# The last batch tile in six output groups, one of them stored through GpSimd's queue on 15 DMA engines

## The chip, the cores and the metric

The kernel runs on one core of one Trainium2 chip. Five engines work beside each other on that core: TensorE (PE) multiplies matrices into PSUM, VectorE (DVE), ScalarE (ACT) and GpSimd (POOL) do elementwise work, and SyncE (SP) here only issues transfers. Sixteen DMA engines move bytes between SBUF and HBM. A transfer is issued by SP, ACT or GpSimd[...].

The metric is the device time of one execution in microseconds (us). The kernel before took 1342.57 us, the median of three runs (1342.16 to 1344.26).

## What is computed

```python
# x: (4096, 32, 64) f32     W: (496, 64, 64) f32     out: (4096, 496, 64) f32
idx_i, idx_j = np.triu_indices(32, k=1)        # the 496 pairs i < j
vi = inputs[:, idx_i, :]
vj = inputs[:, idx_j, :]
vidots = jnp.einsum('bpd,pde->bpe', vi, W)     # one 64x64 matrix for each pair
return vidots * vj
```

For each batch row and each pair (i, j), field i is multiplied by the pair's own matrix and the product is multiplied elementwise with field j. The output is 496 x 64 floats for each of 4096 rows: 520 MB, against 34 MB of input and 8 MB of weights.

## The kernel before

The batch is cut into 32 tiles of 128 rows (tile t is block t // 2, half t % 2). For each tile the 496 pairs go through 46 steps: a step is one field i and up to CH = 16 of its partners j. TensorE writes a step's products into one of four PSUM buffers, then VectorE multiplies them with field j into an output buffer `ot`; for seven of the steps ScalarE copies PSUM out and GpSimd multiplies.

The steps are gathered into groups, and each group has one `ot` buffer and one store. There are three such buffers, so group n can only be written when the store of group n - 3 has landed, on all DMA engines.

```python
    CH = BANK // E2                                             # 16
    p0 = [i * (F - 1) - i * (i - 1) // 2 for i in range(F)]     # first pair of field i
    bounds = [0, p0[3], p0[6] + CH, p0[11], p0[17], NP]         # 0, 90, 187, 286, 391, 496
    groups = list(zip(bounds[:-1], bounds[1:]))                 # 90, 97, 99, 105, 105 pairs
    cap = max(b - a for a, b in groups)
    aside = (1, 3, 5, 7, 9, 11, 13)
    ...
    opool = ctx.enter_context(tc.tile_pool(name="opool", bufs=3))
    psum = ctx.enter_context(tc.tile_pool(name="psum", bufs=4, space=bass.MemoryType.PSUM))
```

Stores go out by SP's queue, one transfer per group: 128 rows, and for each row one contiguous run of pairs (105 pairs are 26,880 bytes). Most loads of x go by ACT's queue. Every third block's load goes by GpSimd's queue instead, in the form that the change takes up: 120 rows in one transfer and the other 8 rows in two more. Small dummy transfers (`turn_engines`) stand between them[...].

```python
    SWR = 120
    ...
    def turn_engines(k: int):
        n = k if k > 1 else 17
        c = used[0] % 8
        used[0] += 1
        src = x[: NB * n].rearrange("(p k) f d -> p k f d", k=NB)
        tc.keep_in_program_order(
            nc.gpsimd.dma_start(out=scratch[:n, :, c : c + 1], in_=src[:, :, 0, 0:1])
        )

    def load_fifteen(blk: int):
        ...
        part(slice(0, SWR), slice(0, F))
        turn_engines(1)
        for h in range(2):
            part(slice(SWR, P), slice(h * F // 2, (h + 1) * F // 2))
    ...
    turn_engines(5)                       # once, at the start
```

The main loop, cut to what the change touches:

```python
    for s, (t, st) in enumerate(sched):
        blk, kt = divmod(t, NB)
        g, i, c0, m = steps[st]           # group, field, first partner, partners
        ...
        base, end = groups[g]
        pa = p0[i] + c0
        if pa == base:
            ots[t] = opool.tile([P, cap, D], F32, tag="ot", name=f"ot_{t}_{g}")
        ot = ots[t]
        ...                               # matmuls into ps
        o = pa - base
        dst = ot[:, o : o + m, :].rearrange("p m (h e) -> p m h e", h=2)
        ...
        if i in aside and c0 == 0 and s not in no_aside:
            tmp = tpool.tile([P, CH, 2, E2], F32, tag="tmp", name=f"tmp_{s}")
            nc.scalar.copy(tmp, src)
            nc.gpsimd.tensor_mul(dst, tmp, xj)
        else:
            nc.vector.tensor_mul(dst, src, xj)
        ...
        if pa + m in ends:
            n0 = ...
            nc.sync.dma_start(
                out=rows_of(out, blk).rearrange("(p k) n d -> p k n d", k=NB)[:, kt, n0 : pa + m, :],
                in_=ot[:, n0 - base : pa + m - base, :],
            )
    turn_engines(11)                      # once, at the end
```

Of the kernel before, what the change touches and what calls it, by code (L numbers as in the profile page):

```python
# [12 lines left out]
def kernel(  # L13
# [16 lines left out]
    nc = tc.nc  # L30

    B, F, D = x.shape
    P = 128
    NB = 2
    assert 2 * D == P and B % (NB * P) == 0
    NBLK = B // (NB * P)
    NP = F * (F - 1) // 2
    E2 = D // 2
    BANK = 512
    CH = BANK // E2  # L40
    RUN = 8
    p0 = [i * (F - 1) - i * (i - 1) // 2 for i in range(F)]


    bounds = [0, p0[3], p0[6] + CH, p0[11], p0[17], NP]
    groups = list(zip(bounds[:-1], bounds[1:]))
    cap = max(b - a for a, b in groups)

    aside = (1, 3, 5, 7, 9, 11, 13)

# [15 lines left out]
    def rows_of(dram: bass.AP, blk: int) -> bass.AP:  # L66
        return dram[blk * NB * P : (blk + 1) * NB * P]

    def new_x(blk: int):

        wide = xpool.tile([P, NB, F * D + 16], F32, tag="xs", name=f"xs_{blk}")
        xs[blk] = wide[:, :, : F * D].rearrange("p k (f d) -> p k f d", d=D)

    def load_x(blk: int, eng, k0: int = 0, k1: int = NB):
        src = rows_of(x, blk).rearrange("(p k) f d -> p k f d", k=NB)
        eng.dma_start(out=xs[blk][:, k0:k1], in_=src[:, k0:k1])
# [4 lines left out]
    SWR = 120  # L81
# [4 lines left out]
# [10 lines that stand above are left out]
        rows = rows_of(x, blk).rearrange("(p k) f d -> p k f d", k=NB)  # L96
        dst = xs[blk]

        def part(ps: slice, fs: slice):
            tc.keep_in_program_order(nc.gpsimd.dma_start(out=dst[ps, :, fs, :], in_=rows[ps, :, fs, :]))  # L100

        part(slice(0, SWR), slice(0, F))
        turn_engines(1)
        for h in range(2):
            part(slice(SWR, P), slice(h * F // 2, (h + 1) * F // 2))


    wflat = w.rearrange("p d e -> p (d e)")
    raw, wT = {}, {}
# [3 lines left out]
    def load_w(c: int, eng=nc.sync):  # L113

        a, b = wrows[c]
        pool, tag = ((opool, "ot"), (opool, "ot"), (const, "w3"), (const, "w3"))[c]
        raw[c] = pool.tile([P, D * D], F32, tag=tag, name=f"raw_{c}")
        eng.dma_start(out=raw[c][: b - a, :], in_=wflat[a:b])

    def order_w(c: int, k: int, copy):  # L120
        r = wrows[c][1] - wrows[c][0]
        rp = tpool.tile([P, EU, 2, D], F32, tag="tmp", name=f"rp_{c}_{k}")
        src = raw[c][:r, :].rearrange("p (d h e) -> p e h d", h=2, d=D)
        copy(rp[:r], src[:, k * EU : (k + 1) * EU])  # L124
        return rp

    def turn_w(c: int, k: int, rp, copy):
        r = wrows[c][1] - wrows[c][0]
        home, tag, n = (wrows[c][0], "w3", r) if c == 3 else (0, "w", wrows[3][0])
        if home not in wT:  # L130
            wT[home] = const.tile([P, n, E2], F32, tag=tag, name=f"wT_{home}")
        pt = psum.tile([P, EU, P], F32, tag="ps", name=f"ptw_{c}_{k}")
        for n in range(EU):
            nc.tensor.transpose(  # L134
                pt[:, n, :r], rp[:r, n].rearrange("p h d -> p (h d)"), ident[:r, :r]
            )
        o = wrows[c][0] - home
        copy(wT[home][:, o : o + r, k * EU : (k + 1) * EU], pt[:, :, :r].rearrange("p e r -> p r e"))  # L138

    def turn_x(blk: int, k: int, q: int, copy):  # L140


        pt = psum.tile([P, RUN // 2, P], F32, tag="ps", name=f"ptx_{blk}_{k}_{q}")
        for u in range(RUN // 2):
            f = q * RUN + 2 * u
            nc.tensor.transpose(  # L146
                pt[:, u, :], xs[blk][:, k, f : f + 2, :].rearrange("p f d -> p (f d)"), ident
            )
        xT = xtpool.tile([P, 2, RUN // 2, P], F32, tag="xT", name=f"xT_{blk}_{k}_{q}")
        copy(xT[:, 0], pt)  # L150
        copy(xT[D:, 1], pt[:D])  # L151
        copy(xT[:D, 1], pt[D:])  # L152
        return xT


    steps = [
        (g, i, c0, min(CH, F - 1 - i - c0))
        for i in range(F - 1)
        for c0 in range(0, F - 1 - i, CH)
        for g, (a, b) in enumerate(groups)  # L160
        if a <= p0[i] + c0 < b
    ]
    NS = len(steps)
    first = {}
    for s, (_, i, _, _) in enumerate(steps):
# [5 lines left out]
    NT = NBLK * NB  # L171
# [36 lines left out]
    v, p, a = nc.vector.tensor_copy, nc.gpsimd.tensor_copy, nc.scalar.copy  # L208
# [8 lines left out]
    ots = {}  # L217
    for s, (t, st) in enumerate(sched):
        blk, kt = divmod(t, NB)
        g, i, c0, m = steps[st]  # L220
        if s in loads:
            new_x(loads[s])
            if loads[s] % 3 == 0:
                load_fifteen(loads[s])
            else:
                load_x(loads[s], nc.scalar)
        for what, *args in due.get(s, ()):
            if what == "x":
                xT[tuple(args)] = turn_x(*args, a)
            elif what == "turn":  # L230
                turn_w(*args, rps.pop(tuple(args)), a)
            else:
                c, k = args
                rps[c, k] = order_w(c, k, (v, v, p, v)[c] if k % 2 == 0 else (v, v, p, a)[c])
                if (c, k) == (2, NU - 1):
                    load_w(3, nc.scalar)

        base, end = groups[g]
        pa = p0[i] + c0
        if pa == base:  # L240
            ots[t] = opool.tile([P, cap, D], F32, tag="ot", name=f"ot_{t}_{g}")
        ot = ots[t]
        ps = psum.tile([P, 2, CH, E2], F32, tag="ps", name=f"ps_{s}")
        for lo, hi in ((0, wrows[3][0]), wrows[3]):
            home, lo, hi = lo, max(pa, lo), min(pa + m, hi)
            if lo < hi:
                for h in range(2):
                    nc.tensor.matmul(  # L248
                        ps[:, h, lo - pa : hi - pa, :],
                        xT[blk, kt, i // RUN][h * D : (h + 1) * D, (i + h) % 2, i % RUN // 2, :],  # L250
                        wT[home][h * D : (h + 1) * D, lo - home : hi - home, :],
                        start=True,
                        stop=True,
                    )
        o = pa - base
        j = i + 1 + c0
        dst = ot[:, o : o + m, :].rearrange("p m (h e) -> p m h e", h=2)
        src = ps[:, :, :m, :].rearrange("p h m e -> p m h e")
        xj = xs[blk][:, kt, j : j + m, :].rearrange("p m (h e) -> p m h e", h=2)
# [7 lines that stand above are left out]
        ends = (p0[2], end) if s < NS and (t, g) == (0, 0) else (end,)  # L267
        if pa + m in ends:
            n0 = p0[2] if len(ends) > 1 and pa + m == end else base
            nc.sync.dma_start(  # L270
                out=rows_of(out, blk).rearrange("(p k) n d -> p k n d", k=NB)[:, kt, n0 : pa + m, :],
                in_=ot[:, n0 - base : pa + m - base, :],
            )
    turn_engines(11)


# [25 lines left out]
```

## Time and profile before

| | |
|---|---|
| time, median of 3 runs | 1342.57 us |
| span of the profiled execution | 1341.7 us |
| busy: PE / DVE / ACT / POOL | 85% / 71% / 35% / 40% |
| bytes moved, mean rate | 562.86 MB, 420 GB/s |
| written to HBM | 520.09 MB |
| share of the 16 DMA engines' time by SP's queue (q1) | 93.0% |
| by ACT's queue (q10) / GpSimd's queue (q0) | 3.8% / 2.0% |
| chain that ended last: DMA / PE / DVE / POOL | 55% / 22% / 14% / 5% |

In the profile's page, the span is cut into 40 equal slices of 33.5 us; a digit is the busy share of a slice in tenths. A transfer is made of packets, and each packet runs on one of the 16 DMA engines. "Landing" is the moment when the last engine of a transfer reports its part as written. The chain is followed back from the last instruction, at each step to whatever released it.

### The profile page before, as it was taken

How to read it: one execution, taken by the hardware profiler on the slowest of the kernel's cores; microseconds unless marked ns; L12 is line 12 of the kernel's file. 1: busy time of each engine (PE TensorE's matmuls, PEld its weight loads, DVE VectorE, ACT ScalarE, POOL GpSimd, SP SyncE). 2: the span in 40 equal slices, each digit the busy share in tenths (PEclk: the TensorE clock that was granted, in tenths of full speed). 3: DMA queues.
4: the chain of work that ended last, by engine and by line, in shares of the span. 5: the costliest groups of instructions: out<-in, count | busy, mean ns of one | idle time of the engine just before them, and what ended most of it. 6: DMA issues, size and time to landing. Idle time of an engine off the chain costs nothing.

```text
span 1341.7 us, 16676 instructions
## 1 busy us (share of the span) xinstructions
PE 1137.5 (85%) x6656; PEld 605.0 (45%) x6656; DVE 954.2 (71%) x1262; ACT 467.7 (35%) x623; POOL 543.0 (40%) x252
## 2 busy tenths in 40 slices
PE   5989888878798797998888988788897879988884
PEld 3545444444344444444444544344444435444442
DVE  4778777767677676776767777577775767777774
ACT  4443333333233342333333333333333323333331
POOL 1723343444334443343453434434334433444441
PEclk9989999989999898998999999899998999999997
DMA  9899999999999999999999999999999999999997
GB/s 383 347 428 419 418 425 427 431 422 430 422 432 431 420 430 421 431 424 432 424 415 430 421 432 426 417 430 408 425 429 429 427 421 428 418 416 431 429 432 320
DMA packets 28895, 562.86 MB, mean 420 GB/s; under 512 B 3537, under 2 KB 3537, under 8 KB 3825
## 3 DMA queue, kind: packets, MB, share of 16 engines
q1 hardware_dynamic: 24176, 530.59, 93.0%
q10 hardware_dynamic: 2576, 20.71, 3.8%
q0 software_dynamic: 2064, 10.50, 2.0%
q8 instruction: 52, 0.85, 0.2%
q14 instruction: 27, 0.21, 0.0%
HBM read 41.68 MB, written 520.09 MB: 419 GB/s over the span
## 4 chain that ended last, share of the span: by engine, by line
DMA 55%; PE 22%; DVE 14%; POOL 5%; issue 2%; ACT 1%; SPq 0%; DVEq 0%; POOLq 0%; ACTq 0%
DMA out_dram<-ot 53%; PE ps L248 20%; DVE ot L265 13%; POOL ot L263 4%; DMA xs<-in_r_inputs_dram 2%; PE ptx L146 2%; ACT tmp L262 1%; PE ptw L134 1%; DVE rp L124 0%; POOL rp L124 0%; ACT xT L150 0%; ACT xT L152 0%; ACT xT L151 0%; DVEq L265 0%; POOL xs L100 0%
## 5 line engine op out<-in xcount | busy, mean ns | idle before, releaser
L265 DVE TENSOR_TENSOR ot<-ps,xs 128x1024 f32<-128x1024 f32 (+15 forms) x1252 | 940.9, 807 | 357.1 <-DMA out_dram<-ot 214.9
L248 PE MATMUL ps<-wT,xT 64*128 64x512 f32 (+13 forms) x6016 | 1046.1, 488 | 167.9 <-DVE ot L265 163.3
L263 POOL TENSOR_TENSOR ot<-tmp,xs 128x1024 f32<-128x1024 f32 x220 | 519.4, 2362 | 770.7 <-ACT tmp L262 592.6
L248 PEld LDWEIGHTS ps<-wT,xT 64*128 64x128 f32 x6016 | 534.7, 195 | 620.3 <-DVE ot L265 372.8
L262 ACT COPY tmp<-ps 128x1024 f32<-128x1024 f32 x220 | 222.7, 1012 | 498.0 <-PE ps L248 462.5
L150 ACT COPY xT<-ptx 128x512 f32<-128x512 f32 x128 | 74.9, 585 | 322.8 <-PE ptx L146 322.8
L146 PE MATMUL ptx<-ident,xs 128*128 128x128 f32 x512 | 84.8, 289 | 13.8 <-DMA xs<-in_r_inputs_dram 8.8
L146 PEld LDWEIGHTS ptx<-ident,xs 128*128 128x128 f32 x512 | 54.2, 142 | 85.9 <-DVE ot L265 60.0
L152 ACT COPY xT<-ptx 64x512 f32<-64x512 f32 x128 | 74.5, 582 | 1.5
L151 ACT COPY xT<-ptx 64x512 f32<-64x512 f32 x128 | 73.9, 577 | 1.5
L134 PE MATMUL ptw<-ident,rp 128*128 128x128 f32 (+1 forms) x128 | 19.1, 304 | 4.8 <-DVE rp L124 4.8
L134 PEld LDWEIGHTS ptw<-ident,rp 128*128 128x128 f32 (+1 forms) x128 | 16.1, 160 | 12.5 <-issue 5.4
L138 ACT COPY wT<-ptw 128x1024 f32<-128x1024 f32 (+1 forms) x15 | 14.8, 984 | 20.0 <-PE ptw L134 16.1
L124 DVE COPY rp<-raw 128x1024 f32<-128x1024 f32 (+1 forms) x9 | 12.8, 1453 | 10.6 <-DMA raw<-in_L_rec_W_dram 10.6
L100 POOL DMA_DIRECT2D xs<-in_r_inputs_dram x15 | 9.5, 636 | 0.0
L124 POOL COPY rp<-raw 128x1024 f32<-128x1024 f32 x4 | 8.0, 1990 | 0.1
L124 ACT COPY rp<-raw 112x1024 f32<-112x1024 f32 (+1 forms) x3 | 5.8, 1949 | 4.6 <-POOL ot L263 2.7
L92 POOL DMA_DIRECT2D scratch<-in_r_inputs_dram x7 | 6.2, 888 | 0.3 <-issue 0.3
L138 DVE COPY wT<-ptw 128x1024 f32<-128x1024 f32 x1 | 1.2, 1224 | 2.5 <-PE ptw L134 2.5
L150 ACT ACT_TABLE_LOAD x1 | 1.3, 1283 | 0.7 <-PEq L289 0.7
masks.py:199 POOL TENSOR_SCALAR_AFFINE_SELECT ident<-ident 128x128 f32<-128x128 f32 x1 | 0.3, 292 | 0.1
masks.py:197 POOL MEMSET ident<- 128x128 f32 x1 | 0.2, 204 | 0.3 <-POOLq L289 0.3
(4 smaller groups left out, 0.4 us busy)
## 6 DMA issues: line engine op xcount, KB each, us to landing
out_dram<-ot SPq DMA_DIRECT2D x64, 3360.0 KB, 16.4
out_dram<-ot SPq DMA_DIRECT2D x32, 3168.0 KB, 15.9
out_dram<-ot SPq DMA_DIRECT2D x32, 3104.0 KB, 17.0
out_dram<-ot SPq DMA_DIRECT2D x31, 2880.0 KB, 16.9
xs<-in_r_inputs_dram ACTq DMA_DIRECT2D x9, 2048.0 KB, 25.4
xs<-in_r_inputs_dram POOLq DMA_DIRECT2D x5, 1920.0 KB, 25.0
raw<-in_L_rec_W_dram SPq DMA_DIRECT2D x3, 2048.0 KB, 13.8
xs<-in_r_inputs_dram SPq DMA_DIRECT2D x2, 1024.0 KB, 10.3
```

Of the source, the lines that this page charges most:

```text
L100: tc.keep_in_program_order(nc.gpsimd.dma_start(out=dst[ps, :, fs, :], in_=rows[ps, :, fs, :]))
L124: copy(rp[:r], src[:, k * EU : (k + 1) * EU])
L134: nc.tensor.transpose(pt[:, n, :r], rp[:r, n].rearrange("p h d -> p (h d)"), ident[:r, :r])
L138: copy(wT[home][:, o : o + r, k * EU : (k + 1) * EU], pt[:, :, :r].rearrange("p e r -> p r e"))
L146: nc.tensor.transpose(pt[:, u, :], xs[blk][:, k, f : f + 2, :].rearrange("p f d -> p (f d)"), ident)
L150: copy(xT[:, 0], pt)
L151: copy(xT[D:, 1], pt[:D])
L152: copy(xT[:D, 1], pt[D:])
L248: nc.tensor.matmul(ps[:, h, lo - pa : hi - pa, :], xT[blk, kt, i // RUN][h * D : (h + 1) * D, (i + h) % 2, i % RUN // 2, :], wT[home][h * ...
L262: nc.scalar.copy(tmp, src)
L263: nc.gpsimd.tensor_mul(dst, tmp, xj)
L265: nc.vector.tensor_mul(dst, src, xj)
```

## The change

Only the last of the 32 tiles is altered. Its pairs are cut into six groups instead of five: 90, 97 and 99 pairs as before, then 55, 100 and 55 in place of 105 and 105. The fifth group, of 100 pairs, is stored by GpSimd's queue instead of SP's, in two transfers: rows 0 to 119, which are to fall on 15 DMA engines, and rows 120 to 127, one row on each of 8. It is meant to leave out of the larger part the one DMA engine that lags behind the rest, as the loads of every third block do. Each row goes as two runs of 50 pairs, so that its pieces are near in size to those of the 55-pair stores; to keep the two runs apart, the second half is written one pair further on in the buffer. [...]

```diff
+    last = [*bounds[:4], p0[13] + CH, p0[21], NP]
+    last_groups = list(zip(last[:-1], last[1:]))
+    HALVED = 4
+    half = p0[17] - last[HALVED]
+    assert last[HALVED + 1] == p0[17] + half
     cap = max(b - a for a, b in groups)
+    assert 2 * half + 1 < cap
 ...
+    def store_fifteen(dram: bass.AP, ot: bass.AP):
+        dst = dram.rearrange("p (c n) d -> p c n d", c=2)
+        src = ot[:, : 2 * half + 2, :].rearrange("p (c n) d -> p c n d", c=2)[:, :, :half, :]
+        for rows in (slice(0, SWR), slice(SWR, P)):
+            tc.keep_in_program_order(nc.gpsimd.dma_start(out=dst[rows], in_=src[rows]))
 ...
-        g, i, c0, m = steps[st]
+        g, i, c0, m = (last_steps if t == NT - 1 else steps)[st]
 ...
-        base, end = groups[g]
+        base, end = (last_groups if t == NT - 1 else groups)[g]
+        halved = (t, g) == (NT - 1, HALVED)
 ...
-        o = pa - base
+        o = pa - base + (halved and pa - base >= half)
 ...
-            nc.sync.dma_start(
-                out=rows_of(out, blk).rearrange("(p k) n d -> p k n d", k=NB)[:, kt, n0 : pa + m, :],
-                in_=ot[:, n0 - base : pa + m - base, :],
-            )
-    turn_engines(11)
+            dram = rows_of(out, blk).rearrange("(p k) n d -> p k n d", k=NB)[:, kt, n0 : pa + m, :]
+            if halved:
+                store_fifteen(dram, ot)
+                turn_engines(4)
+            else:
+                nc.sync.dma_start(out=dram, in_=ot[:, n0 - base : pa + m - base, :])
```

## The prediction

> **What bounds the kernel now.** I read the busy times first, then the slices, then the end of the chain, then the stretches of the last 40 us.
>
> ```profile
> PE 1137.5 (85%) x6656; PEld 605.0 (45%) x6656; DVE 954.2 (71%) x1262; ACT 467.7 (35%) x623; POOL 543.0 (40%) x252
> ...
> DMA  9899999999999999999999999999999999999997
> GB/s 383 347 428 419 418 425 427 431 422 430 422 432 431 420 430 421 431 424 432 424 415 430 421 432 426 417 430 408 425 429 429 427 421 428 418 416 431 429 432 320
> ```
>
> No compute engine is full, but the DMA digit is 9 in nearly every slice at about 425 GB/s: the store of 520 MB sets the pace, and the only slack that a change in the last tile can reach lies in the last slice, at 320 GB/s. If that slice (33.5 us) ran at 425 GB/s it would be about 8 us shorter, part of which is the last latency and teardown. That is already below 2% of the time (26.9 us).
>
> The stretches of the end say how the slack is spread over the engines (columns: start and end, length, five engines, clock, DMA share, GB/s):
>
> ```profile
> 1324.50:1325.30 0.80, 0.00 (x0) 0.00 (x0) 0.00 (x0) 0.00 (x0) 0.00 (x0) 1.00 0.71 302
> 1325.30:1333.20 7.90, 0.00 (x0) 0.00 (x0) 0.00 (x0) 0.00 (x0) 0.00 (x0) 0.51 0.98 419
> 1333.40:1336.20 2.80, 0.00 (x0) 0.00 (x0) 0.00 (x0) 0.00 (x0) 0.00 (x0) 0.50 0.11 48
> 1336.40:1339.50 3.10, 0.00 (x0) 0.00 (x0) 0.00 (x0) 0.00 (x0) 0.00 (x0) 0.50 0.06 26
> 1339.60:1341.70 2.10, 0.00 (x0) 0.00 (x0) 0.00 (x0) 0.00 (x0) 0.00 (x0) 0.50 0.02 4
> ```
>
> From 1325.3 to 1333.2 all 16 DMA engines carry the last store; then the share is 0.11, two engines of 16, and from 1336.4 it is 0.06, a single one. Put packet to packet, the trace gives the same: the last store's data ends between 1333.26 and 1334.19 on fourteen engines, at 1336.28 on one, and at 1339.53 on the last, called B here. B is 6.2 us behind the crowd. The 26,880-byte packet takes 996 ns on B too, so B isn't slow at the end: it brought the lag along. Hence the purpose of the change: give B less.
>
> The chain shows what else hangs on B:
>
> ```profile
> 1299.26 17.00 DMA out_dram<-ot
> 1316.26 0.03 issue
> 1316.29 0.05 DVEq L265
> 1316.34 0.04 issue
> 1316.39 7.86 DVE ot L265 x13
> 1324.25 0.13 DVEq L298
> ```
>
> The store of the 97 pairs (187 less 90) lands at 1316.26 because B ends its part at 1315.75; the others were through by about 1311. Only then is a buffer free for the fifth group, VectorE fills it until 1324.38, SP issues at 1324.41, and the first packet runs at 1325.29, 0.88 us later. The crowd ends the fourth group's 105 pairs at 1324.5 to 1325.7, so it hardly idles. B runs from 1315.75 through three stores without a gap: 23.78 us to 1339.53.
>
> [...] in each of the five split loads one engine gets only completion packets of 4 bytes where 15 get sixteen 8,192-byte packets each. Across the load at 1176, B's lag on the stores falls from about 5 to about 3 us, so the engine left out is B. [...] I take it that B is left out again, and that B is the first of the 8 engines of the second part.
>
> [...] In the split loads 8,192-byte packets of q0 stand between q1's stores, so two queues share an engine and neither stops. [...]
>
> ```profile
> 1172.19 0.78 POOL L100 DMA_DIRECT2D xs<-in_r_inputs_dram  x1
> 1172.97 0.98 POOL L92 DMA_DIRECT2D scratch<-in_r_inputs_dram  x1
> ...
> 1314.08 0.59 POOL L92 DMA_DIRECT2D scratch<-in_r_inputs_dram  x1
> ```
>
> The first q0 packet of the load issued at 1172.19 runs at 1175.74, 3.55 us later; the three loads before it need 3.5, 3.6 and 3.9, the very first 5.2. The dummy transfer of 1314.08 shows its first packet at 1316.51, 2.4 us later. The measured figures are used.
>
> **The change part by part.** Nothing before 1308.8 alters. I write times on the profile's scale.
>
> Packets: 23,040 bytes take 855 ns and 26,880 take 996, so 36.7 ns per KB (1,000 bytes) and some 9 ns fixed. A row of 55 pairs (14,080 bytes) is 526 ns, half a row of 100 pairs (12,800 bytes) 479 ns.
>
> 1. Fourth group, 55 pairs. Its buffer is free at 1308.76 as before, its last product is GpSimd's of 1311.79 to 1314.15, so its store goes out some 1.2 us sooner than the 105 pairs did. Crowd: eight packets, 4.2 us after the 99 pairs (ended 1316.4 to 1317.8): through at about 1320.6 to 1322. B: 99 pairs end at 1323.55 as before, then 4.2 us: 1327.8.
> 2. Fifth group, 100 pairs. It still waits for the landing at 1316.26. VectorE: 2, 16, 1, 16, 15, 14, 13, 12 and 11 pairs, at 0.28, 1.22, 0.21, 1.22, 1.15, 1.09, 1.01, 0.95 and 0.88 us (rows of the same shapes), 8.01 in sum; successive ones overlap by 0.077 each (the fourteen before add up to 9.07 and took 7.99), so 7.4 us: 1316.39 to 1323.8.
> 3. GpSimd's issue: about 1323.9; with 3.45 us to the first packet, 1327.35. The load of 120 rows with two runs per row has as many pieces, which is why I take its latency and not the dummy's. The crowd therefore stands idle from about 1321 to 1327.35, where before it waited about half a microsecond. This is the cost of the change.
> 4. Sixth group, 55 pairs. Buffer free when the 99 pairs land, B's 1323.55, landing 1324.07. VectorE's ten steps of 10 to 1 pairs add up to 5.14, less nine overlaps, 4.45 us: 1324.2 to 1328.65; SP's first packet 0.9 us later, 1329.55. It comes before q0 is empty, so it adds work but no gap.
> 5. The end. Engines with 8 rows of the 100 pairs: 16 x 0.479 + 8 x 0.526 = 11.87 us, 1339.2. The seven besides B with a ninth row: 18 x 0.479 + 8 x 0.526 = 12.83 us, 1340.2. B: one row, 0.96, and 4.2 of the sixth group: about 1334. The engine at 1336.28 before is through with its fourth group at 1324.6, and its lag vanishes in the idle stretch.
>
> Before, data ended at 1339.53; after, at 1340.2: about 0.65 us later. Both hang on the same moment, B's 1315.75, and so differ by 23.78 against 24.4 us (0.51 landing, 0.13 to VectorE, 7.4, 0.1 to the issue, 3.45, 12.83) however far B lags. The teardown after the last landing, 1339.99 to 1341.7, stays. Time: 1342.57 + 0.65, or 1343.2 us.
>
> **The rivals.** *The intended gain.* If the lag were simply shared out, sixteen engines would all end near the present mean of 1333.9, 5.6 us sooner: 1337 us. For it speaks that B does get 0.96 instead of 7.7 us. Against it: bytes can be shared only when there are bytes to send, and between 1321 and 1327 there are none for the crowd, as the fifth group's buffer waits for B.
>
> *GpSimd's transfer starts quicker on idle engines.* With the dummy's 2.4 us, data ends at 1339.15: 1342.2 us. [...] Against: the wait for a packet in progress is at most 1 us on one engine, and with fifteen engines the first one opens almost at once.
>
> *GpSimd's path is worse for stores.* Rows of 12,800 bytes are longer than any that q0 carries in this trace; if they are cut smaller or take longer to prepare, or if the landing of a store by q0 is reported later, 1 to 2 us come on top: 1344 to 1345 us.
>
> *B isn't the engine left out.* Then B gets eight rows, 1327.8 + 11.9 = 1339.7, or 1340.6 with nine; no worse than the crowd, and the time is again 1343 us.
>
> **Range and chances.** All ways lie within 1337 and 1345 us. The term with the widest doubt is the 3.45 us, which I think may be 2.4 to 4.5; the three runs of before spread over 2.1 us. So 1341.4 to 1344.9. A step past 2% would need 26.9 us, which the last tile doesn't hold.
>
> **What would show it.** The first q0 data packet of the store near 1327.3 and a hole in the DMA share from about 1321; VectorE's idle stretch before 1316.4, 1.02 us now, some 4 to 5 us longer; seven engines that end last, together, about a microsecond after the others, and B well before them; the chain passing from VectorE's fifth group to a GpSimd transfer. I am wrong if the crowd's hole is under 4 us, or if B still ends last.

## The result, and the profile after

The change made the kernel slower: 1355.3 us (median of 4 runs, 1354.19 to 1357.18) against 1343.04 us (median of 4, one run more than the prediction had), a ratio of 1.0093 with a 95% interval of 1.0078 to 1.0108. The forecast was 1343.2 us, so 12.1 us were missed; nearly all of them lie in the last 25 us of the program.

The slices of the page after, in the same form as those shown of before (40 slices, here of 33.9 us each):

```profile
DMA  8999999999999999999999999999999999999996
GB/s 372 356 428 419 422 423 426 426 427 431 424 432 427 423 428 423 431 421 431 424 416 430 425 430 428 424 420 409 430 421 431 423 426 424 410 425 433 430 423 176
```

The first 39 slices show nothing new. The last one has dropped from 320 to 176 GB/s, while the busy digit fell only from 7 to 6. Engines that are busy and yet move little: that is the finding, and the stretches of the end show it closer (start and end, length, five engines, clock, DMA share, GB/s):

```profile
1316.00:1320.00 4.00, 2.60 (x12) 1.77 (x14) 2.78 (x4) 0.00 (x0) 0.00 (x0) 0.77 0.94 399
1320.00:1324.00 4.00, 4.00 (x20) 1.93 (x20) 2.93 (x3) 1.57 (x3) 0.00 (x0) 0.80 0.52 222
1324.00:1327.60 3.60, 3.35 (x26) 1.75 (x24) 3.60 (x6) 0.17 (x1) 1.30 (x2) 1.00 0.09 39
1327.60:1331.60 4.00, 2.16 (x20) 1.35 (x20) 2.71 (x8) 0.00 (x0) 0.64 (x2) 1.00 1.05 225
1331.60:1335.60 4.00, 0.00 (x0) 0.00 (x0) 0.00 (x0) 0.00 (x0) 0.00 (x0) 0.53 0.95 186
1335.60:1339.60 4.00, 0.00 (x0) 0.00 (x0) 0.00 (x0) 0.00 (x0) 0.00 (x0) 0.50 1.06 287
1339.60:1343.60 4.00, 0.00 (x0) 0.00 (x0) 0.00 (x0) 0.00 (x0) 0.00 (x0) 0.50 0.87 262
1343.60:1347.60 4.00, 0.00 (x0) 0.00 (x0) 0.00 (x0) 0.00 (x0) 0.00 (x0) 0.50 0.67 245
1347.60:1351.60 4.00, 0.00 (x0) 0.00 (x0) 0.00 (x0) 0.00 (x0) 0.00 (x0) 0.50 0.19 68
```

Up to 1327.6 this is what was forecast: the crowd of DMA engines runs dry from about 1321 and waits for the 100 pairs. From 1327.6 the share is 1.05 and 0.95 (of 16 engines), but the rate is 225 and 186 GB/s. Before, a share of 0.98 was 419 GB/s. The packet records give the reason: of the first 123 packets of 12,800 bytes, those started within 7.6 us, the median takes 0.99 us, not 0.48. Only eight of them take 0.48 to 0.51 us, and put end to start those lie on one engine, with four slower ones between. The other fourteen engines run at half speed. The last data ends at 1351.57, 23.9 us after the first packet; the forecast had 12.83 us for this stretch.

The chain and GpSimd's instructions ahead of that (start, duration, what):

```profile
1317.05 0.30 DVE ot L282
1317.36 0.04 issue
1317.40 4.38 PE ps L265 x16
1321.78 0.59 PE ptx L159 x4
1322.37 2.70 PE ps L265 x16
```

```profile
1326.30 1.35 POOL L118 DMA_DIRECT2D out_dram<-ot  x2 [10.55 <-DVE ot L282]
```

The fifth group starts at 1317.05, when the 97 pairs have landed on the lagging engine B (0.7 us later than in the trace of before). GpSimd issues the store at 1326.30, and its first packet runs at 1327.65. B is left out of the larger part, as planned: when it ends its fourth group at 1328.48, a string of 4-byte packets follows, and then two packets of 12,800 bytes, its one row of the second part, until 1330.41.

### The profile page after: what moved, and what is told of

It is laid out like the page before. It is cut to its first block, busy times and chain, and to the rows that moved or that the text cites. A ratio compares the mean times of both kernels' runs of the same rounds, so it can differ in the third digit from the quotient of the medians.

```text
span 1354.2 us, 16680 instructions
## 1 busy us (share of the span) xinstructions
PE 1142.3 (84%) x6656; PEld 610.0 (45%) x6656; DVE 955.7 (71%) x1262; ACT 467.9 (35%) x623; POOL 544.6 (40%) x254
## 4 chain that ended last, share of the span: by engine, by line
DMA 55%; PE 21%; DVE 12%; POOL 4%; issue 2%; ACT 2%; DVEq 0%; SPq 0%; POOLq 0%; ACTq 0%
DMA out_dram<-ot 55%; PE ps L265 19%; DVE ot L282 11%; POOL ot L280 4%; PE ptx L159 2%; ACT tmp L279 1%; PE ptw L147 1%; ACT xT L165 0%; ACT xT L163 0%; ACT xT L164 0%; DVE rp L137 0%; POOL rp L137 0%; DVEq L282 0%; POOL xs L107 0%; SPq L292 0%
## 5 line engine op out<-in xcount | busy, mean ns | idle before, releaser
L137 DVE COPY rp<-raw 128x1024 f32<-128x1024 f32 (+1 forms) x9 | 12.8, 1453 | 10.6 <-DMA raw<-in_L_rec_W_dram 10.6
```

## The experiments

The theory after the result, called P: some rows, stored by two engines at the same time, are stored at half speed by each, whichever queue issues the transfer. Fourteen engines at 0.99 us a packet and one at 0.48 would be seven pairs and one engine alone; this is the author's estimate from these counts. The packets carry no row, so the trace doesn't show which rows make a pair. One detail fits pairs too: the packets of the one fast engine took 0.62, 0.94 and 0.81 us from 1328.22 on and 0.50 us again at 1330.59, and in just that time, from 1328.58 to 1330.41, B carried its one row of 120 to 127. The rivals: GpSimd's queue is slow for stores as such (Q); fifteen engines at once are slow (F); the regrouping costs the time.

**One transfer of 128 rows instead of 120 + 8.**

```diff
-        for rows in (slice(0, SWR), slice(SWR, P)):
-            tc.keep_in_program_order(nc.gpsimd.dma_start(out=dst[rows], in_=src[rows]))
+        tc.keep_in_program_order(nc.gpsimd.dma_start(out=dst, in_=src))
 ...
-                turn_engines(4)
+                turn_engines(11)
```

> The changed kernel with one edit: the 100 pairs go out by GpSimd's queue in one transfer of 128 rows on all 16 engines, instead of 120 + 8 rows. [...] P expects packets of 0.48 us, the store's data through in about 8 us on the crowd, and a time of 1342 to 1346 us. Theory Q (queue): stores by GpSimd's queue run at half speed as such. Q expects packets of about 1 us again and a time of 1353 to 1357 us.

Measured: 1343.44 us against 1343.4 for the kernel before beside it, ratio 1.0002 (0.9994 to 1.0011). 236 of the 256 packets take under 0.52 us, their mean is 0.49 us, and the data ends at 1340.01. The stretches of this run, same columns:

```profile
1324.00:1327.60 3.60, 3.41 (x26) 1.75 (x22) 3.60 (x6) 0.38 (x1) 1.09 (x2) 1.00 0.09 39
1327.60:1331.60 4.00, 2.31 (x20) 1.50 (x20) 2.92 (x9) 0.00 (x0) 0.28 (x1) 1.00 0.99 410
1331.60:1335.60 4.00, 0.00 (x0) 0.00 (x0) 0.00 (x0) 0.00 (x0) 0.00 (x0) 0.56 0.98 415
1335.60:1339.60 4.00, 0.00 (x0) 0.00 (x0) 0.00 (x0) 0.00 (x0) 0.00 (x0) 0.50 1.06 446
```

The same queue, the same bytes, the same hole ahead, and 410 GB/s where the changed kernel has 225. Q falls. The split into 120 + 8 rows costs 11.9 us (1355.3 less 1343.4, between two sets of runs), nearly all of the loss.

**Regrouping alone, everything by SP's queue.**

```diff
-        halved = (t, g) == (NT - 1, HALVED)
+        halved = False
```

(The dummy transfer at the end is again `turn_engines(11)`, as before.)

> Regrouping alone: the changed kernel's six groups in the last tile, but the 100 pairs go by SP's queue in one 128-row transfer like every other group. It prices the hole that the smaller groups leave on the DMA engines. Theory H (the hole is hidden behind the lagging engine): 1342 to 1345 us, all packets at full speed. A rival, that the regrouping itself costs the 12 us because the fifth and sixth group wait too long for buffers: 1350 us or more.

Measured: 1343.12 us against 1343.4, ratio 0.9996 (0.9987 to 1.0005). The hole is there, as the DMA share shows, and it costs nothing:

```profile
1320.00:1324.00 4.00, 4.00 (x19) 1.93 (x18) 2.46 (x4) 1.06 (x2) 0.00 (x0) 0.66 0.42 180
1324.00:1327.60 3.60, 3.42 (x28) 1.93 (x24) 3.60 (x5) 0.68 (x2) 0.00 (x0) 1.00 0.36 154
1327.60:1331.60 4.00, 2.62 (x24) 1.51 (x22) 3.23 (x9) 0.00 (x0) 0.00 (x0) 1.00 0.96 410
```

In this run the last store lands within half a microsecond on all sixteen engines (median 1339.66, last 1340.11), where before the last was 6.3 us behind. The crowd has lost in the hole about what B lagged by. So the regrouping removes the visible lag and no time.

**Fifteen engines on rows 32 to 91, and fifteen on rows 0 to 59.** Two runs that differ in which 60 rows GpSimd's queue stores, four rows to each of 15 engines; the remaining 68 rows follow by SP's queue behind the sixth group. That the first set should hold no pair and the second seven was an assumption of the author's, which no run had shown.

```diff
-        for rows in (slice(0, SWR), slice(SWR, P)):
-            tc.keep_in_program_order(nc.gpsimd.dma_start(out=dst[rows], in_=src[rows]))
+        tc.keep_in_program_order(nc.gpsimd.dma_start(out=dst[32:92], in_=src[32:92]))
 ...   # after the sixth group's store:
+    for rows in (slice(0, 32), slice(92, 124), slice(124, 128)):
+        tc.keep_in_program_order(nc.sync.dma_start(out=dst_src[0][rows], in_=dst_src[1][rows]))
```

> GpSimd's queue, 15 engines, four rows each, rows 32 to 91 of the 100 pairs; the other 68 rows follow by SP's queue after the sixth group's store. [...] Theory P: all 15 engines at about 0.48 us a packet, the 60 rows through some 4 us after the first packet. Theory Q (GpSimd's queue slow for stores) and theory F (fifteen engines at once are slow): about 1 us a packet, some 8 us.

The other has `dst[0:60]` by GpSimd and rows 60 to 63 and 64 to 127 by SP. (In both the dummy transfer is `turn_engines(12)`.)

> As the run on rows 32 to 91, but rows 0 to 59: again GpSimd's queue, 15 engines, four rows each, the same bytes. [...] Theory P: 14 engines at about 1 us a packet and one at 0.48; the 60 rows through some 8 us after the first packet, twice the other run. Theories Q and F: no difference between the two runs.

Measured, in the first 4 us from the first packet of each, rows 32 to 91:

```profile
1328.20:1332.20 4.00, 2.20 (x20) 1.40 (x20) 2.75 (x8) 0.00 (x0) 0.03 (x1) 1.00 1.01 416
```

and rows 0 to 59:

```profile
1326.75:1330.75 4.00, 2.20 (x20) 1.40 (x20) 2.75 (x8) 0.00 (x0) 0.03 (x1) 1.00 0.99 224
```

Compute is identical to the hundredth, the DMA share is 1 in both, and the rates are 416 and 224 GB/s. Packets take 0.49 us (median; 112 of 120 under 0.52) in the one and 0.97 us in the other, where exactly eight packets, one engine's share, are under 0.52. The 60 rows are through in 4.2 and in 10.1 us, the latter longer than the 8 us of P because the sixth group's packets come between. In DRAM the two sets of rows have the same layout, shifted by 32 rows, so it is likelier the reading side that tells them apart (not tried by itself). Q and F both fall. P holds in this: which rows are stored at the same time decides between 0.49 and 0.97 us a packet. By what rule rows slow each other, two sets can't show. Each of the two is a single run; the 23 runs of the kernel before beside them differ by 0.2%, the packets here by a factor of two. (The times, 1351.12 and 1353.7 us, contain SP's late remainder; its packets, read from SBUF in transfers of 32 or of 64 rows and one of 4, have means of 0.93 and 0.86 us.)

**The same 120 + 8 rows by SP's queue.**

```diff
-            tc.keep_in_program_order(nc.gpsimd.dma_start(out=dst[rows], in_=src[rows]))
+            nc.sync.dma_start(out=dst[rows], in_=src[rows])
```

(The dummy transfer at the end is `turn_engines(11)`.)

> The changed kernel, but its two transfers of 120 and 8 rows are issued by SP's queue instead of GpSimd's. Theory P [...]: the packets of 12,800 bytes take about 1 us again on 14 of 15 engines, and the time is 1347 to 1355 us. Theory Q (GpSimd's queue is slow for this form): about 0.48 us a packet and 1343 to 1346 us.

Measured: 1354.13 us, a single run; median packet 0.98 us. Its stretches:

```profile
1327.60:1331.60 4.00, 0.57 (x8) 0.36 (x6) 1.03 (x5) 0.00 (x0) 0.00 (x0) 0.86 0.96 209
1331.60:1335.60 4.00, 0.00 (x0) 0.00 (x0) 0.00 (x0) 0.00 (x0) 0.00 (x0) 0.50 0.98 232
```

Half speed again, without GpSimd. The form of the transfer does it, with either queue.

**Why was the first packet so early?** In the changed kernel it came 1.35 us after the issue, not 3.45. The kernel before, with the fourth group's store (one transfer of 128 rows) moved to GpSimd's queue, issues it while the engines are still full:

```diff
-            nc.sync.dma_start(
+            by_gp = (t, g) == (NT - 1, 3)
+            store = (nc.gpsimd if by_gp else nc.sync).dma_start(
 ...
```

> The kernel before (five groups), with the last tile's fourth group, 105 pairs, stored by GpSimd's queue in one transfer of 128 rows; nothing else. It goes out while the DMA engines still carry the 99 pairs. Theory L (a GpSimd transfer is late because the engines have SP's packets ahead of it): its first packet some 2.4 to 3.6 us after the issue, as in the split loads, not 1.3 us as on idle engines. Rival: the latency follows the number of pieces, and 128 single rows need 1.3 us here too. Packets of 26,880 bytes at 1 us [...], time 1342 to 1346 us.

```profile
1315.81 0.61 POOL L271 DMA_DIRECT2D out_dram<-ot  x1 [1.85 <-DVE ot L265]
```

Its first q0 packet of 26,880 bytes runs at 1316.99, 1.18 us after the issue; the time of this single run is 1342.53 us. Theory L falls. The rival's rule, more pieces, more delay, explains little: 120 pieces took 1.25 us, 240 took 1.35. What separates the numbers at hand is the direction, loading or storing. Loads by GpSimd's queue show 3.5 to 3.9 us (5.2 the first time) and loads by ACT's queue 2.6 to 4.3 in the trace of before, while stores by GpSimd show 1.2 to 1.35 and the last one by SP 0.88. Why loads are later wasn't tried.

**Less lag instead of a cure at the end.** One more split load, on the kernel before:

```diff
-            if loads[s] % 3 == 0:
+            if loads[s] % 3 == 0 or loads[s] == 14:
                 load_fifteen(loads[s])
```

> The kernel before with one more of its loads in the split form that leaves the lagging engine out: block 14's as well as 3, 6, 9, 12 and 15. [...] Theory P with the lag as the end's limit: the lag of the last engine at the end falls from 6.3 us to 2 to 3, where another engine that lags by 3 us takes over; time 1339 to 1341.5 us. Rival: the sixteenth of the load that goes to the other engines, [...] eats the gain; time within 1 us of before.

Measured: 1341.71 us against 1343.22, ratio 0.999 (0.9983 to 0.9996; 21 and 25 runs): a gain of 1.5 us, just short of the 1339 to 1341.5 us that were expected. In its trace the stores between 1128 and 1166 have a last engine 5.3 to 5.4 us behind the median, against 6.3 to 7.2 before; so the lag moved, but far less than 4 us. At the end two engines are late instead of one:

```profile
1333.20:1336.00 2.80, 0.00 (x0) 0.00 (x0) 0.00 (x0) 0.00 (x0) 0.00 (x0) 0.50 0.13 58
1336.00:1338.00 2.00, 0.00 (x0) 0.00 (x0) 0.00 (x0) 0.00 (x0) 0.00 (x0) 0.50 0.09 40
```

The share of 0.13 is two engines of 16, and they land at 1338.23 and 1338.40, 5.5 and 5.6 us after the median. The second one was 3.0 us behind in the trace of before. So the lag at the end, 5.6 us against 6.3, did not fall to 2 to 3. Nor did block 15's split load do here what it did before: across it the last engine's lag fell from 6.2 to 3.1 us in the trace of before, and from 6.0 to 5.5 in this one. The gain of 1.5 us stands, but that it comes from less lag isn't shown, and a single trace doesn't say how often the lag is so.

## Why the prediction was wrong, by its steps

**What bounds the kernel, and that B sets the end:** right. With B out of the larger part, its last store landed first of all, at 1340.7, and the others at 1342.1 to 1352.1. B itself was some 6 us behind its forecast of 1334, in part because the packets of its sixth group took up to 2.18 us. One reading was off and did no harm: across the load at 1176, B's lag fell from 6.2 to 3.1 us by the landings, not from about 5 to about 3.

**Step 1, the fourth group:** right. SP issued it at 1315.77, straight after GpSimd's product; it landed at 1322.2 on the median engine and at 1329.0 on B.

**Step 2, 7.4 us of VectorE:** too small. The group took from 1317.05 to about 1326.0, 8.95 us. The 5.6 us of idling before it, 4.6 more than before as forecast, left TensorE with full PSUM buffers (it waited 4.4 us for VectorE up to 1317.40); after that VectorE waited for matmuls four times (0.17 to 0.40 us, as the waits name it):

```profile
1317.05 1.55 DVE L282 TENSOR_TENSOR ot<-ps,xs 128x128 f32<-128x128 f32 x3 [5.62 <-DMA out_dram<-ot]
1320.37 1.16 DVE L282 TENSOR_TENSOR ot<-ps,xs 128x960 f32<-128x960 f32 x1 [0.38 <-PE ps L265]
1323.32 7.00 DVE L282 TENSOR_TENSOR ot<-ps,xs 128x832 f32<-128x832 f32 x13 [0.40 <-PE ps L265]
```

The sum assumed that products were always ready. TensorE was also clocked lower just then: 0.77 and 0.80 in the stretches from 1316 to 1324 above, where the trace of before has 1.00:

```profile
1316.00:1324.00 8.00, 6.59 (x48) 3.48 (x44) 7.61 (x13) 0.79 (x2) 0.00 (x0) 1.00 1.00 429
```

What lowered the clock isn't shown. The run with 128 rows has 0.50 and 0.77 from 1316 to 1324 and loses no time in all, so this isn't where the 12 us went.

**Step 3, 3.45 us to the first packet:** too large; it took 1.35 us. The number came from loads, and the stores here were quicker. By luck it made up for step 2: with the 0.7 us that this trace began the group later, step 3 forecasts 1328.0, and 1327.65 was measured.

**Step 4:** the sixth group's store was issued at 1330.34, 1.0 us later than the forecast with the same shift. That is small beside the 11.4 us by which the last data came late.

**Step 5 failed:** "Engines with 8 rows of the 100 pairs: 16 x 0.479 + 8 x 0.526 = 11.87 us". The count of packets was right and the duration wrong. In the store of 128 rows a packet takes the 0.479 us (0.485 in the median); in that of 120 rows it takes 0.97 to 0.99 on fourteen of the fifteen engines. With 0.97 the sum would be 16 x 0.97 + 8 x 0.526 = 19.7 us. The last engine took 23.9, as the sixth group's packets were slowed too (0.71 us in the mean instead of 0.526), and the eight rows of the second part come on top, two packets each; these two weren't priced apart. In the run with 128 rows the step as forecast holds: 12.2 us from the first packet (1327.85) to the last data (1340.01). The split loads, the same form in the other direction, gave no warning: their packets of 8,192 bytes take 0.309 us in the median, 26.5 bytes per ns, as fast as 12,800 bytes in 0.479. There stores stand between the packets: in the load that runs from 1175.74 to 1194.93, 240 packets of 0.325 us in the mean make about four at a time, where the store of 120 rows has fifteen. So two engines of a pair would seldom move their rows at once (argued from these counts, not tried by itself).

**The idle hole:** right, in place and price; the regrouping alone measures 0.9996. So is the reasoning that B's landing at 1316 ties both kernels to the same end.

**The rivals:** the third, "GpSimd's path is worse for stores", pointed the right way for the wrong reason, and its 1 to 2 us were far off. That the engines of one transfer could slow each other was not among them, and the range rested on the claim that all ways lay within 1337 and 1345 us, while 1355.3 was measured.

**The signs:** the hole and the first packet were seen as named; seven engines ending together were not seen, as the last stores of the fifteen besides B land all the way from 1342 to 1352; the chain, against the forecast, ended with VectorE's sixth group, and SP's store of that group landed last of the stores, at 1352.14 (GpSimd's two at 1349.42 and 1351.93).

## What to carry to other kernels

A busy share of 1 with half the bytes (1.05 at 225 GB/s, against 0.98 at 419) was the sign here that DMA engines slow one another: read the rate beside the share, and one packet's duration beside its size. Before leaving an engine out of a transfer, measure what its packets take with the very rows it will store; 60 rows from 32 to 91 and 60 rows from 0 to 59 are the same transfer but for that, and ran at 416 and 224 GB/s. And the idle hole in the crowd was free here, because the laggard set the end anyway; by the same argument curing the laggard inside that hole should gain nothing, which no run tried by itself.

## What the runs showed of the hardware that wasn't expected

Some packets ran at a quarter of the speed, not at half. In the changed kernel, while the sixth group's store met the 100 pairs, nine packets took 1.83 to 2.21 us. B's packet of 14,080 bytes from 1331.56 took 2.18 us and one of 12,800 bytes beside it 1.99 us, both 6.4 bytes per ns, while most others went on at 12.8. Two at 6.4 and one at 12.8 make 25.6, near the 26.7 bytes per ns of a packet at full speed (12,800 in 0.479 us). That three engines share in this way is an estimate from these sums; it is read from a few packets and wasn't tested.

Which of the sixteen engines lags stays open. In the run with 120 rows by SP's queue, fourteen engines start on the 100 pairs from 1325.19 to 1325.46, and the fifteenth at 1325.81, just as the engine that is last with the fourth group ends it (1325.82). The packets carry no engine's number, but by this fit the lagging engine took part there: the same 120 rows left it out by GpSimd's queue and not by SP's.
